# Graph attention on one core: query rows ordered by their number of edges

## The chip, the core and the metric

The kernel runs on one core of a Trainium2 chip. The core has a matrix engine (TensorE, in the profile PE, with its weight loads as PEld), a vector engine (VectorE, DVE), a scalar engine (ScalarE, ACT), a general engine (GpSimd, POOL), an engine that only issues transfers here (SyncE, SP) and 16 DMA engines. Each engine works through its own queue of instructions in order; semaphores tie the queues together. The metric is the device time of one execution in microseconds (us), taken as the median of several runs. Less is better.

## The reference

One layer of graph attention with a residual and a layer norm, all in float32. x is 16 x 1024 x 512: 16 batches of 1024 nodes. adj is one 1024 x 1024 matrix of zeros and ones that all batches share. With 8 heads of 64 columns:

```python
q, k, v = (x @ Wq + bq), (x @ Wk + bk), (x @ Wv + bv)      # each split into 8 heads of 64
scores = einsum('bqhd,bkhd->bhqk', q, k) / 8
scores = scores + (1.0 - adj) * -1e9                       # only edges count
out = einsum('bhqk,bkhd->bqhd', softmax(scores), v)
y = x + out @ Wo + bo
y = (y - mean(y)) / sqrt(var(y) + 1e-5)                    # over the 512 columns
```

adj is sparse and uneven: 4043 edges in all, up to 66 in one row, and 60 rows with none (such a row attends to all nodes alike).

## The kernel before

**Edges instead of a dense matrix.** The kernel doesn't compute all scores. It puts 128 query rows on the 128 partitions (a tile; 8 tiles, t = 0 to 7, in a batch) and works in blocks of one edge per partition. A block gathers, for each partition, the key and value row of that edge (`kvg`, 4 KB a row, an indirect DMA from POOL out of `kv_rows` in device memory), multiplies query and key (`products`, DVE), reduces each head's 64 products (`scores`, DVE), takes the exponential (`exponentials`, ACT) and multiplies the value row by it (`weigh`, on ACT as eight instructions or on DVE as one, as `by_act` says).

**Two kinds of block.** A tile's *own* blocks (OWN[t] of them) hold one edge of each of its own 128 queries, so the query tile `qt` serves them all, and the weighted rows are added in place on DVE (`add_own`). Rows with more edges leave a remainder. These are packed, 128 to a *shared* block (BLOCKS[t] of them); there each partition's query row has to be gathered as well (`qg`, a second indirect DMA), and a 0/1 matrix (`sums`) adds the rows to their queries by two matmuls (`add_up`, TensorE). A batch has 21 own and 15 shared blocks, 36 in all, 576 in the run. `normalise` adds the two sums, divides by the sum of exponentials, and the result is transposed.

**Everything else.** For each batch `pair` computes q, k and v for two tiles at a time on TensorE (k and v by seven products in place of eight, with weights prepared in T1 to T4) and stores them as rows (`q_rows`, `kv_rows`, three batches deep). `norm` squares q and k per head on ACT and keeps the sums: at the end `guard` checks with them that the exponentials, which are taken without subtracting a maximum, stayed within LIMIT, and otherwise a plain program recomputes all. `finish` takes a tile through the output product, adds x (`load_y`) and bo (on POOL), takes mean and variance (the power on POOL) and stores the rows.

**Order.** The order of each engine's instructions is written out by a loop over steps, one block a step (n). At step n it gathers block n + 8, multiplies block n + 4 and reduces it, takes the exponential of block n + 3, weighs block n + 2 (ACT) or n + 1 (DVE) and adds block n. TensorE's other work, and the work that follows from it, is handed out by a credit (`share`) worked out from the costs PRODUCT, SUM and TRANSPOSE, so that every step gets an equal part of it. 34 steps (LEAD_IN) run before block 0; in them the weights are prepared and the edge lists made (`edges`, one list per tile, started at the steps EDGES_FROM). After the last q, k and v, ten tiles' attention results that were put aside (SPILL) are brought back and finished.

**Queues.** SP issues the plain transfers: x, the stores of q and kv rows, `qt` (128 contiguous rows of `q_rows`), `y` (128 rows of x again) and the output rows. POOL issues the indirect ones: `kvg` and `qg`. In its queue also stand the bias addition on `y` and the power of the variance.

The functions that the change touches, with their callers:

Of the kernel before, what the change touches and what calls it, by code (L numbers as in the profile page):

```python
# [16 lines left out]
HEADS = 8  # L17
EPS = 1e-5
NEG = 1e9
LIMIT = 28.0  # L20
# [3 lines left out]
OWN = (7, 3, 3, 1, 1, 2, 2, 2)  # L24
BLOCKS = (5, 2, 1, 2, 2, 1, 1, 1)
DEGREE = (80, 16, 16, 16, 16, 16, 16, 16)

AHEAD = 8
KG_BUFS, QG_BUFS, QT_BUFS, PV_BUFS = 8, 4, 3, 5
# [10 lines left out]
EDGES_FROM = (-33, -30, -18, -14, -10, -5, 0, 5)  # L40
# [111 lines left out]
def kernel(  # L152
# [33 lines left out]

    nc = tc.nc
# [30 lines left out]
    with ExitStack() as main:  # L218
# [6 lines left out]
        def fill_psum(name):  # L225
# [21 lines left out]
            one.tile([P, 2, D], F32, name=name) for name in ("b11", "b21", "b22", "t1", "t2", "t3", "t4")  # L247
# [8 lines left out]
        check = one.tile([P, 2 * NT], F32, name="check")  # L256
        gmax = one.tile([P, 2 * B], F32, name="gmax")

        kv_rows = [dram.tile([N + 1, 2 * D], F32, name=f"kv_rows_{i}") for i in range(ROWS)]
        q_rows = [dram.tile([N, D], F32, name=f"q_rows_{i}") for i in range(ROWS)]  # L260
        spill = [dram.tile([P, D], F32, name=f"spill_{i}") for i in range(len(SPILL))]
# [36 lines left out]
        def bias_setup():  # L298
            bk_bc = work.tile([P, D], F32, tag="y", name="bk_bc", bufs=4)
            broadcast(bk_bc, bk)  # L300
            yield
            n8 = small.tile([P, HEADS], F32, name="bk_norms")
            nc.vector.tensor_tensor(bk_bc, bk_bc, bk_bc, op=OP.mult)
            nc.vector.tensor_reduce(n8, bk_bc.rearrange("p (h d) -> p h d", d=HD), axis=AX.X, op=OP.add)
            nc.vector.tensor_reduce(bk_norm, n8, axis=AX.X, op=OP.max)
# [8 lines left out]
            bvb = work.tile([P, NPAIR, P], F32, tag="y", name="bvb", bufs=4)  # L314
# [19 lines left out]

        def edges(t):
            nb, J, K = BLOCKS[t], DEGREE[t], OWN[t]
            a = work.tile([P, N], F32, tag="kv", name=f"a_{t}", bufs=5)
            nc.sync.dma_start(a, adj[ds(t * P, P), :])
            for _ in range(3):
                yield  # L340
            v = work.tile([P, N], F32, tag="kv", name=f"codes_{t}", bufs=5)
            nc.gpsimd.tensor_tensor(v, a, place[:, 0:N], op=OP.mult)
            st = small.tile([P, 4], F32, name="est")
            deg, end, lim, off = (st[:, i:i + 1] for i in range(4))
            kl = small.tile([P, J + 2], F32, tag=f"kl{J}", name=f"kl_{t}", bufs=2)
            kr = small.tile([P, max(OWN)], F32, tag="kr", name=f"kr_{t}", bufs=2)
            yield

            nc.scalar.activation(a, a, AF.Copy, accum_out=deg)
            nc.scalar.activation(a, a, AF.Square, bias=neg_one, scale=2.0)  # L350
            nc.scalar.activation(a, a, AF.Square, bias=neg_one, accum_out=check[:, t:t + 1])
# [21 lines left out]
            nc.vector.tensor_scalar(deg, deg, -float(K), 0.0, op0=OP.add, op1=OP.max)  # L373
# [6 lines left out]
            nc.vector.tensor_copy(kl[:, J + 1:J + 2], query[:, t:t + 1])  # L380
# [5 lines left out]
            of = work.tile([P, max(BLOCKS) * P], F32, tag="of", name=f"of_{t}", bufs=1)  # L386

            o, span = of[:, 0:nb * P], place[:, 0:nb * P]
# [27 lines left out]
            for i0 in range(0, nb, 4):  # L416
# [7 lines left out]
                )  # L424

# [51 lines left out]
        def norm(b, t, i, s):  # L477
            if t == 0 and i == 0:
                NRM[b] = work.tile([P, 2, NT, HEADS], F32, tag="nrm", name=f"nrm_{b}", bufs=2)
            for h in range(HEADS):  # L480
                sq = work.tile([P, HD], F32, tag="sq", name=f"sq_{b}_{t}_{i}_{h}", bufs=2)
                nc.scalar.activation(sq, s[:, ts(h, HD)], AF.Square, accum_out=NRM[b][:, i, t, h:h + 1])  # L482
# [156 lines left out]
        def load_y(b, t, tag="y", bufs=4):  # L639
            Y[b, t] = work.tile([P, D], F32, tag=tag, name=f"y_{b}_{t}", bufs=bufs)  # L640
            loaded[b, t] = now[0]
            nc.sync.dma_start(Y[b, t], x[b, ds(t * P, P), :])

            if fronts or t % 2:
                later(2 if fronts else 3, lambda: nc.gpsimd.tensor_tensor(Y[b, t], Y[b, t], bo_bc, op=OP.add))  # L645
                biased[b, t] = True

        def reload(b, t, k):
            OT[b, t] = work.tile([P, D], F32, tag="ewg"[k % 3], name=f"oTs_{b}_{t}", bufs=1)
            nc.sync.dma_start(OT[b, t], spill[b * NT + t - SPILL[0]])  # L650
            load_y(b, t, "q", 2)
# [343 lines left out]
```

## Time and profile before

| | us |
|---|---|
| median of three runs (lowest to highest) | 2121.68 (2117.72 to 2123.0) |
| the profiled execution | 2120.32 |
| its span, first to last instruction | 2118.5 |

| engine | busy us | share of the span |
|---|---|---|
| TensorE (PE) | 2034.2 | 96% |
| VectorE (DVE) | 1930.0 | 91% |
| ScalarE (ACT) | 1642.2 | 78% |
| GpSimd (POOL) | 1196.2 | 56% |

The DMA engines moved 583.25 MB. The software queue q0, fed by POOL, took 47.0% of their time, and the hardware queue q1, fed by SP, 31.9%. The mean granted clock of TensorE was 0.987.

How to read it: a busy share is an average over the span; a matmul's end is modelled, so neighbours overlap; a float32 matmul is recorded as two. An indirect DMA on POOL shows the time in which POOL makes it, not the transfer. In a group's row the idle time in front names what ended it. Issues on SP don't count as busy time.

### The profile page before, as it was taken

To read this page: it belongs to the slowest core of one execution; us is meant where nothing else is said; L and a number is where in the kernel's file an instruction comes from. 1 tells how busy PE (TensorE), PEld (TensorE's weight loads), DVE (VectorE), ACT (ScalarE), POOL (GpSimd) and SP (SyncE) were. 2 spreads that over 40 slices of the span, in tenths; PEclk is the share of its full clock that TensorE was granted. 3 is DMA by queue.
4 is the path that set the end of the run, shared out by engine and by line. 5 is a ranking of instruction groups with operands and counts; after the bars stand their busy time and mean duration, and the time that the engine had idled before them with its cause. 6 is when DMAs were issued, how large, how long until landed. Compare 5 with 4: busy or idle time off the path is not lost. (4 is left out here: it accounts for less than half of the span.)

```text
span 2118.5 us, 29525 instructions
## 1 busy us (share of the span) xinstructions
PE 2034.2 (96%) x5933; PEld 1031.0 (49%) x5933; DVE 1930.0 (91%) x3860; ACT 1642.2 (78%) x8132; POOL 1196.2 (56%) x1098
## 2 busy tenths in 40 slices
PE   8897999999999999999999999999999999999677
PEld 3444555454554545545554555555455554554343
DVE  6789999999989899998999999999989989999876
ACT  5477888777878788787877878787887869897665
POOL 2044566655656565565655656465555656566872
PEclk9998999999999999999999999999999999999889
DMA  5367788787978878797887879878787988989883
GB/s 194 110 232 237 266 285 318 265 323 250 337 248 294 286 258 325 241 314 260 279 314 243 324 243 320 281 270 317 243 327 238 329 274 300 325 309 328 284 310 112
DMA packets 219596, 583.25 MB, mean 275 GB/s; under 512 B 34047, under 2 KB 34059, under 8 KB 219406
## 3 DMA queue, kind: packets, MB, share of 16 engines
q0 software_dynamic: 102144, 331.89, 47.0%
q1 hardware_dynamic: 114656, 244.40, 31.9%
q10 hardware_dynamic: 2606, 4.99, 0.7%
q14 instruction: 141, 1.16, 0.2%
q8 instruction: 49, 0.80, 0.1%
HBM read 477.37 MB, written 136.88 MB: 290 GB/s over the span
## 5 line engine op out<-in xcount | busy, mean ns | idle before, releaser
L722 POOL DMA_INDIRECT kvg<-kv_rows,key_row x576 | 641.0, 1113 | 413.0 <-DVE pv L767 132.3
L763 ACT ACTIVATE pv<-kvg,pv 128x64 f32<-128x64 f32 x2624 | 660.7, 338 | 0.2 <-ACT pv L753 0.2
L470 PE MATMUL pq<-wq,xT 128*128 128x512 f32 x1024 | 481.7, 596 | 3.8 <-DVE y L663 3.7
L470 PE MATMUL po<-wo,oT 128*128 128x512 f32 x944 | 431.5, 596 | 0.7 <-ACT oT L811 0.7
L743 DVE TENSOR_REDUCE s<-qk 128x8 f32<-128x512 f32 x576 | 390.8, 678 | 6.4
L716 POOL DMA_INDIRECT qg<-q_rows,query_row x240 | 273.2, 1138 | 76.7 <-issue 62.7
L470 PEld LDWEIGHTS pq<-wq,xT 128*128 128x128 f32 x1024 | 189.3, 191 | 199.3 <-issue 176.8
L470 PEld LDWEIGHTS po<-wo,oT 128*128 128x128 f32 x944 | 179.7, 192 | 201.6 <-issue 189.8
L482 ACT ACTIVATE sq<-q 128x64 f32<-128x64 f32 x1024 | 245.5, 244 | 37.8 <-DVE q L497 37.8
L739 DVE TENSOR_TENSOR qk<-qt,kvg 128x512 f32<-128x512 f32 x336 | 261.0, 777 | 0.0
L676 POOL TENSOR_TENSOR stats<-stats,neg_half 128x1 f32<-128x1 f32 x128 | 88.2, 689 | 288.1 <-DVE stats L675 283.4
L482 ACT ACTIVATE sq<-kv 128x64 f32<-128x64 f32 x1024 | 245.3, 244 | 3.8 <-ACT sq L482 3.1
L586 PE MATMUL x<-b,xT 128*128 128x512 f32 x504 | 238.4, 595 | 0.1
L586 PE MATMUL pp<-t,s 128*128 128x512 f32 x504 | 237.1, 593 | 0.7 <-DVE w L602 0.7
L482 ACT ACTIVATION_READ_ACCUMULATOR sq<-kv 128x1 f32 x1024 | 195.2, 191 | 0.0
L482 ACT ACTIVATION_READ_ACCUMULATOR sq<-q 128x1 f32 x1024 | 194.6, 190 | 0.0
L645 POOL TENSOR_TENSOR y<-y,bo_bc 128x512 f32<-128x512 f32 x116 | 161.5, 1393 | 41.4 <-DMA y<-in_x_dram 40.2
L779 DVE TENSOR_TENSOR pv<-pv,pv 128x520 f32<-128x520 f32 x208 | 179.0, 860 | 0.5 <-ACT pv L763 0.5
L739 DVE TENSOR_TENSOR qk<-qg,kvg 128x512 f32<-128x512 f32 x240 | 174.1, 725 | 5.2 <-issue 4.2
L753 ACT ACTIVATE pv<-s,absent 128x8 f32<-128x8 f32 x336 | 95.8, 293 | 102.3 <-DVE o L796 70.0
L767 DVE TENSOR_TENSOR pv<-kvg,pv 128x512 f32<-128x512 f32 x248 | 174.5, 703 | 0.0
L788 PE MATMUL sum<-pv,sums 128*128 128x256 f32 x480 | 146.7, 388 | 19.0 <-DVE pv L767 14.5
(149 smaller groups left out, 2972.9 us busy)
## 6 DMA issues: line engine op xcount, KB each, us to landing
kv_rows<-kv SPq DMA_DIRECT2D x128, 512.0 KB
x<-in_x_dram SPq DMA_DIRECT2D x128, 256.0 KB
q_rows<-q SPq DMA_DIRECT2D x128, 256.0 KB
qt<-q_rows SPq DMA_DIRECT2D x128, 256.0 KB
y<-in_x_dram SPq DMA_DIRECT2D x128, 256.0 KB
out_dram<-y SPq DMA_DIRECT2D x128, 256.0 KB
kvg<-kv_rows,key_row POOLq DMA_INDIRECT x576
a<-in_adj_dram SPq DMA_DIRECT2D x8, 512.0 KB
```

The costliest lines, as they stand in the source:

```text
L470: nc.tensor.matmul(p, lhs()[:, ts(c, P)], w[:, c, :], start=(c == 0), stop=(c == NPAIR - 1))
L482: nc.scalar.activation(sq, s[:, ts(h, HD)], AF.Square, accum_out=NRM[b][:, i, t, h:h + 1])
L586: nc.tensor.matmul(R[bank], l[:, ts(c, P)], right[:, c, :], start=(first and c == 0), stop=(c == 1), skip_group_check=True,)
L645: later(2 if fronts else 3, lambda: nc.gpsimd.tensor_tensor(Y[b, t], Y[b, t], bo_bc, op=OP.add))
L716: nc.gpsimd.indirect_dma_start(out=QG[n], out_offset=None, in_=q_rows[b % ROWS], in_offset=bass.IndirectOffsetOnAxis(ap=query_row[:, g:g + ...
L722: nc.gpsimd.indirect_dma_start(out=KG[n], out_offset=None, in_=kv_rows[b % ROWS], in_offset=bass.IndirectOffsetOnAxis(ap=key_row[:, g:g + ...
L739: nc.vector.tensor_tensor(QK[n], q, KG[n][:, 0:D], op=OP.mult)
L743: nc.vector.tensor_reduce(S[n], QK.pop(n).rearrange("p (h d) -> p h d", d=HD), axis=AX.X, op=OP.add)
L763: nc.scalar.activation(pv[:, ts(h, HD)], v[:, ds(D + h * HD, HD)], AF.Copy, scale=pv[:, D + h:D + h + 1])
L767: nc.vector.tensor_tensor(pv[:, 0:D].rearrange("p (h d) -> p h d", d=HD), v[:, D:].rearrange("p (h d) -> p h d", d=HD), pv[:, D:, None].to ...
L779: nc.vector.tensor_tensor(PV[b, t], PV[b, t], pv, op=OP.add)
L788: nc.tensor.matmul(PSUM[b, t][:, 0, 0:HD2], m, pv[:, 0:HD2], **kw)
```

## The change

**Order by degree.** A new preparation, `ranks`, loads all eight tiles of adj, sums each row on ACT, ranks the 1024 rows by degree (a row-wide comparison per tile on DVE, with the row number breaking ties), and scatters (row, degree) to its rank in device memory by eight indirect DMAs. Read back, `asked_row[:, t]` names the 128 rows of tile t. From then on a tile is 128 rows of like degree. `edges` gathers its rows of adj by that list, and `qt`, `y` and the output rows, which are no longer contiguous, become indirect DMAs on POOL.

**Other blocks.** OWN becomes (1, 2, 2, 3, 4, 5, 5, 7) and BLOCKS (0, 0, 0, 0, 0, 0, 1, 5): 29 own and 6 shared blocks a batch, 35 in all, 560 in the run. Tiles 0 to 5 have no sum on TensorE, and `normalise` takes their sums as they are. The matrices and offsets are made for two tiles only.

**Norms of pairs.** `norm` takes one sum for two heads, 128 columns, so four ACT instructions with an accumulator in place of eight; the sum of a pair bounds each head's, and LIMIT goes from 28 to 31.

**Smaller edits.** `by_act` gives every second block with i = 0 to ACT in all batches, where before it did so in the first and last only. `qt` and `pv0` get one buffer more, `y` five in place of four; reloaded tiles use the storage of T1 to T4 for y, and up to three of them may be open. The store of the output comes two steps after the last ACT instruction, before it one. The check that adj holds only zeros and ones moves into `checks`, and the value buffers are cleared there.

```diff
-OWN = (7, 3, 3, 1, 1, 2, 2, 2)
-BLOCKS = (5, 2, 1, 2, 2, 1, 1, 1)
-DEGREE = (80, 16, 16, 16, 16, 16, 16, 16)
+OWN = (1, 2, 2, 3, 4, 5, 5, 7)
+BLOCKS = (0, 0, 0, 0, 0, 0, 1, 5)
+DEGREE = (8, 8, 8, 8, 8, 8, 16, 80)
-KG_BUFS, QG_BUFS, QT_BUFS, PV_BUFS = 8, 4, 3, 5
+KG_BUFS, QG_BUFS, QT_BUFS, PV_BUFS, Y_BUFS = 8, 4, 4, 5, 5
-EDGES_FROM = (-33, -30, -18, -14, -10, -5, 0, 5)
+EDGES_FROM = (-14, -13, -12, -10, -8, -4, -6, -15)
...
+        def ranks():
+            for _ in range(2):
+                yield
+            for t in range(NT):
+                ADJ.append(work.tile([P, N], F32, tag="kvg", name=f"adj_{t}", bufs=KG_BUFS))
+                nc.gpsimd.dma_start(ADJ[t], adj[ds(t * P, P), :])
...
+            for t in range(NT):
+                nc.scalar.activation(ADJ[t], ADJ[t], AF.Copy, accum_out=asked[:, t, 1:2])
...
+            for t in range(NT):
+                nc.vector.scalar_tensor_tensor(
+                    keys, row, key[:, t:t + 1], place, op0=OP.is_lt, op1=OP.min, accum_out=rank[:, t:t + 1]
+                )
...
+            for t in range(NT):
+                nc.gpsimd.indirect_dma_start(
+                    out=order_views[t], out_offset=bass.IndirectOffsetOnAxis(ap=rank_row[:, t:t + 1], axis=0),
+                    in_=asked[:, t, :], in_offset=None,
+                )
+            for _ in range(2):
+                yield
+            nc.sync.dma_start(ranked, order.rearrange("(t p) c -> p t c", p=P))
+            yield
+            nc.vector.tensor_copy(asked_row, ranked[:, :, 0])
...
         def norm(b, t, i, s):
...
-            for h in range(HEADS):
-                sq = work.tile([P, HD], F32, tag="sq", name=f"sq_{b}_{t}_{i}_{h}", bufs=2)
-                nc.scalar.activation(sq, s[:, ts(h, HD)], AF.Square, accum_out=NRM[b][:, i, t, h:h + 1])
+            for h in range(NPAIR):
+                sq = work.tile([P, P], F32, tag="sq", name=f"sq_{b}_{t}_{i}_{h}", bufs=2)
+                nc.scalar.activation(sq, s[:, ts(h, P)], AF.Square, accum_out=NRM[b][:, i, t, h:h + 1])
...
         def load_y(b, t, k=None):
...
-            nc.sync.dma_start(Y[b, t], x[b, ds(t * P, P), :])
+            nc.gpsimd.indirect_dma_start(
+                out=Y[b, t], out_offset=None, in_=x_rows,
+                in_offset=bass.IndirectOffsetOnAxis(ap=asked_row[:, t:t + 1], axis=0), element_offset=b * N * D,
+            )
...
                 def norm_out():
                     nc.scalar.activation(y, y, AF.Identity, bias=st[:, 4:5], scale=st[:, 3:4])
-                    later(1, store)
+                    later(2, store)

                 def store():
-                    nc.sync.dma_start(out_ap[b, ds(t * P, P), :], y)
+                    nc.gpsimd.indirect_dma_start(
+                        out=out_rows[b, t], out_offset=bass.IndirectOffsetOnAxis(ap=asked_row[:, t:t + 1], axis=0),
+                        in_=y, in_offset=None, element_offset=b * N * D,
+                    )
...
         def gather(n):
...
-                nc.sync.dma_start(QT[b, t], q_rows[b % ROWS][ds(t * P, P), :])
+                nc.gpsimd.indirect_dma_start(
+                    out=QT[b, t], out_offset=None, in_=q_rows[b % ROWS],
+                    in_offset=bass.IndirectOffsetOnAxis(ap=asked_row[:, t:t + 1], axis=0),
+                )
...
         def by_act(n):
             b, t, i = blocks[n]
-            return 0 < i < OWN[t] or ((b in (0, B - 1) or i >= OWN[t]) and n % 2 == 0)
+            return 0 < i < OWN[t] or n % 2 == 0
...
         def normalise(b, t):
...
+            if BLOCKS[t]:
+                s = PSUM.pop((b, t))
+                nc.vector.tensor_tensor(r, s[:, 1, HD2:HD2 + HEADS], pv[:, D:], op=OP.add)
...
+            else:
+                nc.vector.reciprocal(r, pv[:, D:])
```

## The prediction

> **What bounds the kernel now.** I read the page first: the shares by engine and the forty slices.
>
> ```profile
> PE 2034.2 (96%) x5933; PEld 1031.0 (49%) x5933; DVE 1930.0 (91%) x3860; ACT 1642.2 (78%) x8132; POOL 1196.2 (56%) x1098
> ...
> PE   8897999999999999999999999999999999999677
> ```
>
> TensorE is busy from the third slice to the last three. The busy time of a stretch that leaves out the start and the end, and of the last stretch, came next (columns: stretch, length, busy us and instructions of PE, PEld, DVE, ACT, POOL, then clock, DMA share, GB/s).
>
> ```profile
> 383.00:1757.00 1374.00, 1367.70 (x4020) 695.72 (x4019) 1273.57 (x2488) 1090.59 (x5495) 803.12 (x737) 1.00 0.83 284
> ...
> 1966.00:2079.00 113.00, 80.27 (x215) 40.97 (x214) 95.82 (x230) 79.23 (x279) 79.81 (x81) 0.88 0.83 280
> ```
>
> From 383 to 1757 us eleven batches (2 to 12) take 1374 us, 124.9 each, and TensorE is busy 99.5% of that at full clock: the bound. DVE follows at 93%. In the last batch no engine is full: chains decide. The batch limits are the starts of every 36th reduction of line 743; they give 138 us for batch 0, 115 for batch 1, 109 and 111 for batches 13 and 14, and 142 us from the first reduction of batch 15 to the end.
>
> Third, the groups by form (mean ns of one, then idle before it).
>
> ```profile
> L763 ACT ACTIVATE pv<-kvg,pv 128x64 f32<-128x64 f32 x2624 | 660.7, 338 | 0.2 <-ACT pv L753 0.2
> L722 POOL DMA_INDIRECT kvg<-kv_rows,key_row x576 | 641.0, 1113 | 413.0 <-DVE pv L767 132.3 <-ACT pv L753 97.4 <-issue 82.6
> ...
> L716 POOL DMA_INDIRECT qg<-q_rows,query_row x240 | 273.2, 1138 | 76.7 <-issue 62.7 <-DVE qk L739 11.9 <-DVE s L743 0.9
> ...
> L482 ACT ACTIVATE sq<-q 128x64 f32<-128x64 f32 x1024 | 245.5, 244 | 37.8 <-DVE q L497 37.8
> ...
> L779 DVE TENSOR_TENSOR pv<-pv,pv 128x520 f32<-128x520 f32 x208 | 179.0, 860 | 0.5 <-ACT pv L763 0.5
> ...
> L645 POOL TENSOR_TENSOR y<-y,bo_bc 128x512 f32<-128x512 f32 x116 | 161.5, 1393 | 41.4 <-DMA y<-in_x_dram 40.2
> L789 PE MATMUL sum<-pv,sums 128*128 128x264 f32 x480 | 148.8, 392 | 0.5 <-ACT pv L763 0.5
> L788 PE MATMUL sum<-pv,sums 128*128 128x256 f32 x480 | 146.7, 388 | 19.0 <-DVE pv L767 14.5 <-DVE rden L800 4.5
> ```
>
> Then the waits, and POOL in order of time (start, us, what).
>
> ```profile
> POOL stats L676 <- DVE stats L675: 283.4, 87, 5.2
> ```
>
> ```profile
> 902.84 0.97 POOL L716 DMA_INDIRECT qg<-q_rows,query_row  x1 [0.30 <-issue]
> 904.11 1.48 POOL L722 DMA_INDIRECT kvg<-kv_rows,key_row  x1 [0.30 <-issue]
> 905.90 0.96 POOL L716 DMA_INDIRECT qg<-q_rows,query_row  x1 [0.30 <-DVE pv L779]
> ```
>
> POOL's idle time is mostly waiting because it is early. Back to back, an indirect DMA costs its own 1.12 us plus 0.30 us of gap: 1.42 us. That number decides this case.
>
> **What the Trainium skill says.** Perfetto Trace Analysis, "DMA Instruction — SWDGE (GPSIMD)": such an interval is the generation of descriptors, not the transfer, so the 1.12 us is POOL's own work; the trace agrees, since its packet records, matched in order to the 816 issues, put the last packet at a median 5.0 us (2 KB rows) and 5.5 us (4 KB rows) after the issue. DMA: Bandwidth & Descriptors, "SWDGE vs HWDGE vs iDMA": all these DMAs go through one software queue; here it is q0, 47.0% of the DMA engines. SBUF — State Buffer, "Who interferes with whom": a DVE instruction with two SBUF inputs contends with a GpSimd instruction that reads SBUF. The trace agrees for line 645, which reaches 911.67:
>
> ```profile
> 910.47 1.76 DVE L779 TENSOR_TENSOR pv<-pv,pv 128x520 f32<-128x520 f32 x1
> ...
> 913.42 0.69 DVE L779 TENSOR_TENSOR pv<-pv,pv 128x520 f32<-128x520 f32 x1
> ```
>
> Such stretching adds 113 us to DVE in all, while of 1,937 DVE instructions beside an indirect DMA alone two were stretched. So more indirect DMAs should not slow DVE, and the bias additions stay (118 for 116).
>
> **The change, part by part.**
>
> *TensorE.* Sums go from 15 to 6 blocks a batch. The busy rows give 295.5/240 = 1.23 us a block, but ends are modelled; from the first matmul of a block to the next instruction is 0.88 us (median). I take 0.88, low end of the two: 9 x 0.88 = 7.9 us a batch, 127 us in all. The other end is 11.1. A TensorE-bound batch becomes 124.9 - 7.9 = 117.0.
>
> *DVE.* Products +128 x 0.777 - 144 x 0.725 = -5; weighing -136 x 0.703 = -96; additions +128 x 0.860 = +110; reductions -16 x 0.678 = -11; normalising without a sum in 96 tiles -96 x (0.680 + 0.156) = -80; shorter edge lists and the new ranks about -17. Sum -99: 1831 us, 107 us a batch. Not shown before: the 1024-wide comparison of the ranks; nearest row 1.46 us (L356), 8 of them, in the sum.
>
> *ACT.* 120 more blocks weighed: 960 x 0.252 (660.7/2624, they overlap) = +242. Norms now take 881 us for 2048 squares with their accumulator reads. A 128-wide square isn't in the trace; VectorE: DVE Perf Modes, "The TRN2 errata", prices ACT at 224 cycles plus the width at 1.2 GHz, 0.240 us for 64 (row: 0.244), so 0.29 estimated for 128; by the slope to line 672 (0.717 for 512), 0.31. With the 0.19 read, 1024 x 0.50 = 512: -369. Sum with exponentials -119: 1523 us.
>
> *POOL, where it is paid.* The queries are no longer contiguous rows, so loads of qt and y and stores of out, 128 each, move from SP's hardware queue to indirect DMAs; 144 qg and 16 kvg gathers go. Net +224 x 1.42 = +318 us. A steady batch has 65 such DMAs for 51: 65 x 1.42 + 8 x 1.39 + 8 x 0.69 = 109 us, against 89 of 124.9 before. Still under 117, at 93%. But it is uneven. In the changed order of POOL, steps 0 to 13 hold 21 DMAs, 30 us of work in 47; steps 14 to 34 hold 44 DMAs, 8 biases and 8 powers: 62.5 + 11.1 + 5.5 = 79 us in 21 x 3.34 = 70. POOL ends some 9 us late. It can be 7.7 late: a gather now precedes its reduction by 15.2 us (median), at the least 7.5. Queued behind are the gathers, and DVE's products wait for those. Line 645 also waits for a y now landing 5 us after issue from a late POOL. I take 2.5 us a batch lost: 119.5.
> The scatter of out has no row. Low end 0.97 like the shortest gather; high end 2.16, the longest in the trace, 8 us a batch more, which alone lifts POOL to 117. I take 1.12.
> SP loses 392 issues and keeps x, q_rows and kv_rows, which nothing then delays.
>
> *Costed at nothing.* The fifth y buffer, fourth qt, third pv0 and the store one step later only loosen waits; the columns named "idle before" show none on these tiles. If they are still too few, POOL stands at a y load until the store five tiles back has landed, with the gathers behind it.
>
> *Transfers.* -37.7 MB of qg; kvg rows unchanged, as each edge and each isolated node is one row (4103 a batch). 100 MB move from q1 to q0. Hidden; uncovered, a late gather is the case above.
>
> *Start.* All 4 MB of adj are asked for at once beside 3 MB of wq and wk, wv. The first 17 us now move about 5 MB, near 310 GB/s, so I add 6 us (between 0 and 12: 3.5 MB at that rate is 11). The chain of ranks (eight scatters of 1.4 us, two landings) fits about four lead-in steps; if not, DVE and SP stand a few us at it.
>
> *End.* Batches 13 and 14 run at DVE 95-97%: -6.5 each, -13. Last batch: POOL's order from its first gather to the end holds 34 kvg, 6 qg, 7 qt, 19 y, 31 out, 12 biases, 28 powers. Here I use 1.3 us back to back (the undisturbed 1.0 + 0.3), 0.65 for a power: 126 + 16 + 18 = 160 us, as long as POOL takes now from there (1956.9 to 2118.5), waits not counted. I add 12 (between -7, were POOL hidden, and +30).
>
> Sum on the span of 2118.5: 6 - 13 x 5.4 - 13 + 12 = -65, so 2053; the execution's own time was 2120.3, 1.8 above its span, so **2055 us**. The median of the runs, 2121.7, is 0.06% above that execution.
>
> **Rivals.**
> - *TensorE alone.* POOL's lateness stays within the slack: 117.0 a batch, 4 - 13 x 7.9 - 14 - 7 = -120, 2000 us. For it: 93% is under 100%, and DVE and ACT get lighter in every batch. Against: POOL's heavy 21 steps.
> - *POOL sets the batch (slower).* One cost, the indirect DMA on POOL with what it waits for. 65p + 16.6 = 124.9 at p = 1.67 us, 0.25 above the measured start to start. At 1.85 a batch is 137: +156, and with start and end about 2290. For it: 1.48 and 2.16 us intervals exist, and every y and out adds a wait for a buffer or for ACT. Against: mean 1.12.
> - *Little gained.* POOL at 1.55 to 1.65, or the start and end eat it: 2095 to 2130.
>
> **How the numbers follow.** Forecast (own range 2020 to 2090) 0.45; TensorE alone 0.20; little gained 0.15; POOL sets the batch 0.20. A change of 0.3% (6 us) is about what a measurement can tell. Faster: 0.45 + 0.20 + 0.09 = 0.74; same 0.05; slower 0.21. The range 1990 to 2145 takes in the first three and the nearer part of the POOL case.
>
> **What the profile after would show.** Right: reductions of line 743's kind 117 to 121 us apart every 35; POOL near 70% busy with its waits for the power (283 us now) mostly gone; ACT near 1520, DVE near 1830; idle time of DVE and TensorE behind gathers near each batch's end. Wrong: indirect DMAs longer than 1.25 us in the mean, POOL without idle time, a tail over 160 us, or a first gather much later than 122 us.

## The result: the changed kernel, and its profile

The changed kernel takes 2144.0 us, the median of four runs (2132.54 to 2148.86), against 2119.7 for the kernel before (2117.72 to 2123.0): a ratio of 1.0105, interval 1.0061 to 1.0149. It is 1% slower, and its fastest run is slower than the slowest of the kernel before. The profiled execution took 2142.24 us with a span of 2140.5, 22 us more than the 2118.5 before.

The page of the changed kernel, shares by engine and one of the slice rows:

```profile
PE 1946.7 (91%) x5334; PEld 930.5 (43%) x5334; DVE 1810.1 (85%) x3545; ACT 1686.2 (79%) x7024; POOL 1474.0 (69%) x1350
...
PE   8968999999999999999999999999999999998664
```

TensorE lost 88 us of work and DVE 120, and yet the span grew. The share that rose is POOL's, from 56% to 69%; ACT's rose by one point. The last four slices of the PE row fell from "9677" to "8664".

Windows of the changed kernel: batches 2 to 11, and most of the last stage (columns as before: length, PE, PEld, DVE, ACT, POOL, clock, DMA share, GB/s):

```profile
392.00:1637.00 1245.00, 1189.98 (x3295) 571.73 (x3296) 1083.16 (x2111) 1032.87 (x4359) 900.49 (x811) 0.98 0.79 266
...
1986.00:2110.00 124.00, 76.49 (x174) 34.83 (x173) 91.97 (x212) 88.15 (x314) 99.31 (x104) 0.83 0.68 215
```

TensorE is busy 95.6% of the steady batches, where it was 99.5%, and its clock is 0.98, where it was 1.00: it is still the fullest engine, but now it waits. In the last stage POOL, busy 99 of 124 us with a gap before each of its DMAs, is the fullest engine.

The groups of the changed kernel that answer to the rows shown before:

```profile
L850 ACT ACTIVATE pv<-kvg,pv 128x64 f32<-128x64 f32 x3584 | 902.7, 339 | 1.6 <-remote 1.6
L809 POOL DMA_INDIRECT kvg<-kv_rows,key_row x560 | 638.0, 1139 | 306.5 <-issue 107.4
L793 POOL DMA_INDIRECT qt<-q_rows,asked_row x128 | 144.7, 1130 | 35.9 <-issue 35.0
L767 POOL DMA_INDIRECT out_dram<-y,asked_row x128 | 144.8, 1132 | 34.7 <-issue 22.1
L720 POOL DMA_INDIRECT y<-in_x_dram,asked_row x128 | 143.2, 1118 | 32.0 <-issue 31.7
L557 ACT ACTIVATE sq<-q 128x128 f32<-128x128 f32 x512 | 150.7, 299 | 13.7 <-DVE q L572 13.4
```

The durations are those of the prediction: 1.12 to 1.14 us for every kind of indirect DMA, the scatter of `out` included. No kind of instruction on POOL became clearly dearer (`kvg` rose most, from 1.113 to 1.139 us).

The waits of the changed kernel (who waited, for whom; us in all, times, longest):

```profile
POOL stats L757 <- DVE stats L756: 78.4, 38, 5.0
DVE y L744 <- POOL y L726: 62.8, 27, 6.2
DVE qk L826 <- DMA kvg<-kv_rows,key_row: 46.3, 12, 7.3
DVE stats L760 <- POOL stats L757: 46.1, 33, 6.3
```

The direction has turned. Before, POOL stood 283 us at the power, waiting for DVE; now 78. And DVE, which stood 10.5 us at a power and 9.9 at a bias addition in the kernel before,

```profile
DVE stats L679 <- POOL stats L676: 10.5, 8, 3.9
DVE y L663 <- POOL y L645: 9.9, 4, 5.4
```

stands 46 and 63, and 46 more at gathered rows.

Where the 22 us lie, by stages. The limits are the starts of every 36th reduction of scores (every 35th in the changed kernel), "start" is the time of the first and "last" is from the first reduction of batch 15 to the end of the span.

| us | start | batch 0 | batch 1 | batches 2 to 12, each | batch 13 | batch 14 | last |
|---|---|---|---|---|---|---|---|
| before | 130.2 | 138.0 | 115.3 | 124.9 | 108.5 | 110.9 | 141.8 |
| changed | 141.7 | 137.6 | 113.5 | 124.0 | 103.6 | 125.8 | 153.9 |
| difference | +11 | 0 | -2 | -0.9 | -5 | +15 | +12 |

The forecast had +6, -5.4 in each of batches 0 to 12, -6.5 in each of 13 and 14, and +12. Two terms are far off: the steady batch (-12 in all instead of -70) and batch 14.

### The profile page after: what moved, and what is told of

It is laid out like the page before. It is cut to its first block, busy times and chain, and to the rows that moved or that the text cites. A ratio compares the mean times of both kernels' runs of the same rounds, so it can differ in the third digit from the quotient of the medians.

```text
span 2140.5 us, 26366 instructions
## 1 busy us (share of the span) xinstructions
PE 1946.7 (91%) x5334; PEld 930.5 (43%) x5334; DVE 1810.1 (85%) x3545; ACT 1686.2 (79%) x7024; POOL 1474.0 (69%) x1350
## 5 line engine op out<-in xcount | busy, mean ns | idle before, releaser
L850 ACT ACTIVATE pv<-kvg,pv 128x64 f32<-128x64 f32 x3584 | 902.7, 339 | 1.6 <-remote 1.6
L826 DVE TENSOR_TENSOR qk<-qt,kvg 128x512 f32<-128x512 f32 x464 | 355.6, 766 | 52.4 <-DMA kvg<-kv_rows,key_row 43.7
L753 ACT ACTIVATE ysq<-y,stats 128x512 f32<-128x512 f32 x128 | 91.9, 718 | 113.9 <-DVE stats L749 107.9
L793 POOL DMA_INDIRECT qt<-q_rows,asked_row x128 | 144.7, 1130 | 35.9 <-issue 35.0
L767 POOL DMA_INDIRECT out_dram<-y,asked_row x128 | 144.8, 1132 | 34.7 <-issue 22.1
L720 POOL DMA_INDIRECT y<-in_x_dram,asked_row x128 | 143.2, 1118 | 32.0 <-issue 31.7
L557 ACT ACTIVATE sq<-q 128x128 f32<-128x128 f32 x512 | 150.7, 299 | 13.7 <-DVE q L572 13.4
L557 ACT ACTIVATE sq<-kv 128x128 f32<-128x128 f32 x512 | 150.6, 299 | 0.0
L661 PEld LDWEIGHTS x<-b,xT 128*128 128x128 f32 x504 | 96.0, 193 | 118.7 <-issue 109.1
L661 PEld LDWEIGHTS pp<-t,s 128*128 128x128 f32 x504 | 95.0, 192 | 110.3 <-issue 101.9
```

Source lines behind the costliest of these rows:

```text
L557: nc.scalar.activation(sq, s[:, ts(h, P)], AF.Square, accum_out=NRM[b][:, i, t, h:h + 1])
L661: nc.tensor.matmul(R[bank], l[:, ts(c, P)], right[:, c, :], start=(first and c == 0), stop=(c == 1), skip_group_check=True,)
L720: nc.gpsimd.indirect_dma_start(out=Y[b, t], out_offset=None, in_=x_rows, in_offset=bass.IndirectOffsetOnAxis(ap=asked_row[:, t:t + 1], axi ...
L767: nc.gpsimd.indirect_dma_start(out=out_rows[b, t], out_offset=bass.IndirectOffsetOnAxis(ap=asked_row[:, t:t + 1], axis=0), in_=y, in_offse ...
L793: nc.gpsimd.indirect_dma_start(out=QT[b, t], out_offset=None, in_=q_rows[b % ROWS], in_offset=bass.IndirectOffsetOnAxis(ap=asked_row[:, t: ...
L826: nc.vector.tensor_tensor(QK[n], q, KG[n][:, 0:D], op=OP.mult)
```

## The steady batch: what eats 7 us

TensorE's work allows 117.0 us a batch and the batch takes 124.0. The trace offers two suspects. They meet at the border between two batches, where DVE stands longest. The steps (one reduction to the next, means over batches 2 to 12) show it: they are 1.9 to 5.1 us long, but the one into a new batch takes 7.9 us, with DVE busy for 2.9 of them. POOL in order of time at such a border of the changed kernel, with the DVE instruction it ends at:

```profile
1386.75 1.02 POOL L809 DMA_INDIRECT kvg<-kv_rows,key_row  x1 [1.28 <-DMA kv_rows<-mean]
1388.07 1.24 POOL L793 DMA_INDIRECT qt<-q_rows,asked_row  x1 [0.31 <-issue]
1389.62 1.00 POOL L809 DMA_INDIRECT kvg<-kv_rows,key_row  x1 [0.30 <-ACT pv L850]
1390.93 1.00 POOL L809 DMA_INDIRECT kvg<-kv_rows,key_row  x1 [0.30 <-ACT sq L557]
1391.96 0.58 POOL L757 TENSOR_TENSOR stats<-stats,neg_half 128x1 f32<-128x1 f32 x1
1392.51 1.26 POOL L726 TENSOR_TENSOR y<-y,bo_bc 128x512 f32<-128x512 f32 x1
1392.57 1.23 DVE L760 TENSOR_TENSOR stats<-stats 128x1 f32<-128x1 f32 x1 [3.36 <-POOL stats L757]
```

The first gather of the new batch waits for that batch's last row (`kv_rows<-mean`); three DMAs follow with only the usual 0.30 us between them, and the power and the bias addition stand behind them. DVE waits 3.36 us for the power, and what stands behind it in DVE's queue waits with it.

- **Late rows.** A gather is asked for eight steps before its block. In the kernel before, the new batch's rows are complete nine steps ahead; in the changed one six to seven. The constant `EARLY` (11 steps), from which `share` sets how far TensorE's q, k and v work runs ahead, is the same in both, but the work between is not. So the first gathers of a batch leave late and in a bunch. They precede their reductions by 7.5, 8.2, 9.4 and 8.7 us in the mean (before: 14.0, 14.3, 20.6 and 16.1).
- **A full POOL.** 90 us busy a batch, and 65 gaps of 0.30 us before a DMA, make 109 of 124. A bunch that has formed has little room in which to dissolve.

**A second place.** DVE's longest stand isn't yet TensorE's loss. TensorE itself stands 5.2 us of each steady batch, and 2.1 of them lie at the border, in its step and the eight after it. Another 2.5 lie in the middle of the batch, between the 18th and the 20th reduction, and there it is one wait, the largest in total that TensorE has in this run:

```profile
PE pxT L516 <- DVE y L744: 27.5, 10, 4.7
```

One of the ten, with the DVE instruction that ends it and the POOL instruction before that:

```profile
824.96 1.27 POOL L726 TENSOR_TENSOR y<-y,bo_bc 128x512 f32<-128x512 f32 x1
...
826.26 0.69 DVE L744 SCALAR_TENSOR_TENSOR y<-po,y 128x512 f32<-128x512 f32 x1 [2.38 <-POOL y L726]
...
827.02 1.12 PE L516 MATMUL pxT<-ident,x 128*128 128x128 f32 x4 [4.69 <-DVE y L744]
```

In all ten the `y` of DVE begins 0.03 to 0.04 us after POOL's bias addition has ended, and POOL had made that addition straight after an indirect DMA or a power, without idle time. So the full queue shows here too, but what comes late is a bias, not a gather.

The experiments take away late rows, POOL's work, both, or neither but something that only looks like them.

### Rows earlier: EARLY 14, then EARLY 13

```diff
-EARLY = 11
+EARLY = 14
```

> The changed kernel with EARLY 14 in place of 11: TensorE's q, k and v of the next batch are planned three steps earlier, so that their rows are complete 9 steps before the batch's first block and not 6, and its first gathers go out 8 steps ahead and not 5 or 6. POOL has the same instructions. Theory 1 (POOL's queue is too full whatever the order): within 10 us of the changed kernel's 2144. Theory 2 (the rows of the next batch come too late, so that its first gathers are bunched and DVE stands some 5 us in the last step of each batch): about 5 us in each of 12 batches comes back, 2080 to 2095.

2108.14 us, ratio 0.9955 (0.9938 to 0.9972). This kernel leaves out the end of the last tile (one output store of 128), so only its steady batches are used: 121.1 us each, against 124.0. That is less than the second theory asked for (2080 to 2095), but part of the 7 us is the late rows. With 13 steps nothing is left out:

```diff
-EARLY = 11
+EARLY = 13
```

> The changed kernel with EARLY 13 alone, the bias still on POOL; rows of the next batch complete 8 steps ahead. If the late rows and POOL's work are separate costs that add up: 1.2 us a batch back, as between the two kernels with the bias on DVE (117.9 and 116.7): about 2128. If the late rows only hurt because POOL is full: more, 121 to 122 us a batch, 2105 to 2120.

2086.97 us, ratio 0.9854 (0.9836 to 0.9872), more than expected: one constant turns 1% slower into 1.5% faster. A steady batch takes 118.4 us. DVE's waits in this kernel:

```profile
DVE stats L760 <- POOL stats L757: 66.0, 46, 4.8
DVE y L744 <- POOL y L726: 64.7, 24, 4.2
DVE qk L826 <- DMA kvg<-kv_rows,key_row: 10.5, 14, 2.2
```

The wait for gathered rows fell from 46.3 to 10.5 us, and the two waits for POOL's own work did not fall. So the 5.6 us a batch did not come from a quicker power or bias. TensorE's idle time falls from 5.2 to 1.9 us a batch: at the border from 2.1 to 0.1, and at the wait for DVE's `y` from 2.5 to 0.4, although DVE stands at the bias almost as long as before (46 us in batches 2 to 12, in the changed kernel 53). Why TensorE is then so seldom behind it isn't shown. Why 14 does worse than 13 in the steady batches stays open too; with 14, TensorE idles 3.1 us a batch, 0.2 of them at the border.

### POOL relieved: bias additions on DVE

```diff
-            if fronts or t % 2:
+            if False:
                 later(2 if fronts else 3, lambda: nc.gpsimd.tensor_tensor(Y[b, t], Y[b, t], bo_bc, op=OP.add))
```

DVE then adds bo itself, with an instruction more for each of those tiles.

> The changed kernel with the addition of bo to y done by DVE (a second instruction in the output step, 0.6 us) and not by POOL. POOL loses 118 instructions of 1.35 us, DVE its 45 us of waits for them in batches 2 to 11 and the stretching beside them, and gains about 80 us of work. Theory 1: POOL has 10 us a batch less, 2090 to 2115. Theory 2: the late rows stay, 2135 to 2150.

2055.17 us, ratio 0.9691 (0.9672 to 0.971), far better than either theory had it. A steady batch takes 117.9 us. The rows are as late as in the changed kernel: DVE still waits 42.9 us for gathered rows and still stands at the border. TensorE's wait in the middle of the batch is gone, and its idle time is 1.2 us a batch, 1.1 of them at the border. So taking 10.8 us (8 x 1.35) from POOL does as much as bringing the rows earlier, although it puts 0.7 us an instruction on DVE.

### POOL relieved further: plain transfers

```diff
-                nc.gpsimd.indirect_dma_start(
-                    out=QT[b, t], out_offset=None, in_=q_rows[b % ROWS],
-                    in_offset=bass.IndirectOffsetOnAxis(ap=asked_row[:, t:t + 1], axis=0),
-                )
+                nc.sync.dma_start(QT[b, t], q_rows[b % ROWS][ds(t * P, P), :])
```

and likewise for `y` and `out`: the three streams go back to SP's queue. That leaves out the order of the query rows in these three, while blocks and edge lists stay as they are, so the work on every other engine is that of the changed kernel.

> The changed kernel with qt, y and the output rows as plain transfers on SP again, as in the kernel before: 24 indirect DMAs a batch leave POOL. Left out: the order of the query rows (a tile's qt, x and output rows are those of the plain order, beside edge lists of the new order), the bytes are the same. Theory 1: POOL falls from 109 to 75 us a batch, TensorE's 117 us a batch become the bound, and what is left of the loss is the start (11 us): 2000 to 2025. Theory 2: with 5 or 6 steps of lead, 16 us or more, the gathers are late only because they are bunched; without POOL's other DMAs at most half of the 5 us a batch comes back and nothing else: 2100 to 2120. If neither POOL nor the order of gathers is the cause (TensorE's clock, or the dependence of DVE and ACT on each other with more own blocks): 2130 to 2145.

2031.05 us, ratio 0.9579 (0.9563 to 0.9595), 6 us above the range of the first theory. A steady batch takes 118.4 us, no less than with the bias alone, and not the 117 of that theory. The last stage takes 127.6 us instead of 153.9: here is where the additional DMAs on POOL do cost time of their own.

### Both: bias on DVE and EARLY 13

```diff
-EARLY = 11
+EARLY = 13
...
-            if fronts or t % 2:
+            if False:
```

> The changed kernel with the bias addition on DVE and EARLY 13 (the rows of the next batch complete 8 steps ahead, first gathers 7). With the bias on DVE alone batches 2 to 11 took 117.9 us each, and DVE still stood 35 us at gathered rows in eleven batches. If the late rows are what remains: 117.0 a batch, TensorE's own time, and 2040 to 2050. If the two causes are one (once POOL has room, 5 steps of lead do): 2050 to 2060, no difference.

2048.8 us, ratio 0.9674 (0.9656 to 0.9692), the fastest of the kernels that compute all: 3.3% below the kernel before and 4.4% below the changed one (2048.8/2144.0). A steady batch takes 116.7 us. Window of its steady batches:

```profile
392.00:1600.00 1208.00, 1207.16 (x3426) 587.64 (x3425) 1118.00 (x2267) 1063.16 (x4505) 818.86 (x755) 1.00 0.84 285
```

TensorE is busy 1207 of 1208 us at full clock: the bound of 117.0 that the prediction worked out is reached and holds. Nothing lies below it: all of it together, plain transfers, bias on DVE and EARLY 13, gives the same.

> The changed kernel with the bias on DVE, EARLY 13, and qt, y and the output rows as plain transfers on SP. Left out: the order of the query rows (plain rows beside edge lists of the new order; the bytes are the same). POOL has 41 indirect DMAs a batch, 61 us of work. If TensorE is the only bound of the steady batches that is left: 116.5 to 117 a batch, no better than with POOL's 98 us, and all the gain over 2049 is in the last two batches, 25 to 40 us: 2005 to 2025. If POOL still costs something in the steady batches: below 116 a batch.

2007.63 us, ratio 0.9481 (0.9464 to 0.9499), 116.5 us a steady batch with POOL at 541 of 1208 us. POOL is early again: it stands 273 us at the power, waiting for DVE.

Against the kernel with both and indirect DMAs, the remaining time (44 us of span) lies mostly at the end: 231.9 us for batch 14 and the last stage, against 267.8.

| steady batch, us | step into a new batch | DVE idle in it | TensorE idle in the batch | batch |
|---|---|---|---|---|
| changed | 7.9 | 5.0 | 5.2 | 124.0 |
| EARLY 14 | 4.3 | 0.3 | 3.1 | 121.1 |
| EARLY 13 | 5.7 | 1.5 | 1.9 | 118.4 |
| plain transfers | 6.7 | 4.0 | 1.5 | 118.4 |
| bias on DVE | 6.6 | 4.2 | 1.2 | 117.9 |
| bias on DVE, EARLY 13 | 4.3 | 1.1 | 0.3 | 116.7 |
| the same, plain transfers | 3.3 | 0.2 | 0.2 | 116.5 |

(The steps are those that end batches 2 to 12.) The batch follows TensorE's idle time and not DVE's stand at the border: with the bias on DVE, or with plain transfers, that stand stays nearly whole, and the batch is short all the same; with EARLY 14 it is almost gone, and the batch is longer than with 13.

Undoing one cause gains 5.6 or 6.1 us, undoing both 7.4. They do not add, and could not, since about 116.5 us is TensorE's own time; either one alone takes away three quarters of the loss. That fits a loss which needs both, late rows and a queue too full to work the bunch off. The last of the controls below says the same from another side.

### Is it POOL's time, or that DVE depends on the bias?

The bias on DVE takes away two things: POOL's time, and DVE's wait for POOL's addition (62.8 us). This kernel gives the time back without the dependence: POOL fills a spare tile that nobody reads.

```diff
-            if fronts or t % 2:
-                later(2 if fronts else 3, lambda: nc.gpsimd.tensor_tensor(Y[b, t], Y[b, t], bo_bc, op=OP.add))
-                biased[b, t] = True
+            if (fronts or t % 2) and now[0] > 20:
+                later(2 if fronts else 3, lambda: [nc.gpsimd.memset(before, 0.0) for _ in range(SPARE)])
```

> The changed kernel with the bias addition on DVE, and nine memsets of a spare 128 x 128 tile at the place on POOL where it stood, for which nothing waits (1.0 to 1.5 us in all, to be read from the trace). If it is POOL's time that the bias takes from the gathers: back to 122 to 126 us a batch, 2110 to 2150. If it is DVE waiting for the bias and being held up beside it: it stays at 118 a batch, 2050 to 2070.

2205.31 us, ratio 1.0412 (1.0391 to 1.0433), and 128.0 us a steady batch. One such filling, in the order of time:

```profile
945.73 2.31 POOL L727 MEMSET before<- 128x128 f32 x9
```

It came out longer than the addition it stands for, 2.3 us in the mean against 1.35, so it puts some 18 us a batch on POOL where the bias put 10.8. So time on POOL costs by itself, with nothing waiting for the filling. How much of the 6.1 us it explains isn't settled: a straight line from 117.9 (none) to 128.0 (18) passes 10.8 at 123.9, and the changed kernel has 124.0, but no run with 10.8 shows that the line is straight, and in the changed kernel's trace TensorE's largest wait hangs on the bias. DVE now waits at the power instead:

```profile
DVE stats L760 <- POOL stats L757: 180.7, 73, 12.9
```

### More time for the power

```diff
-                later(3, shift)
-                later_last(4, norm_out)
+                later(5, shift)
+                later_last(6, norm_out)
```

> The changed kernel with DVE's use of the power two steps later (the shift at step 5 and ACT's last instruction at step 6 after the output product, not 3 and 4). POOL's work is the same, only DVE no longer waits for a power that stands behind gathers. Theory 1, if the waits for small POOL results are the larger part of it: 2115 to 2130; if the late gathers are: 2135 to 2150, as theory 2 has it.

2147.94 us, ratio 1.0132 (1.0115 to 1.0149): no gain. A steady batch takes 123.7 us, and the end grows. Giving DVE's read of the power two steps more does not help while POOL's queue itself is late. DVE's waits only move: in batches 2 to 12 it stands 71.6 us at the bias, where it stood 53 in the changed kernel. The first gathers of a batch lead their reductions by 7.0 to 9.1 us, as in the changed kernel.

### Controls: one part at a time on the kernel before

The bias additions on DVE, in the kernel before:

```diff
-            if fronts or t % 2:
+            if False:
```

> The kernel before with the bias addition on DVE, a control: there TensorE is busy 99.5% of batches 2 to 12 and POOL has 35 us a batch to spare. All theories of POOL: within 0.3% of 2119, since only DVE's work grows, from 113 by about 5 less the stretching of up to 6 us a batch. If the bias on POOL hurt in itself, whatever POOL's load: faster, 2070 to 2100.

2108.64 us, ratio 0.9946 (0.9929 to 0.9964). I expected no difference, and there is a small gain of 11 us, told of at the end. It lies between the two ranges, and is an eighth of what the same edit gains in the changed kernel (89 us), so the large gain belongs to the change.

The three streams as indirect DMAs in the kernel before, with its own blocks and row order:

```diff
-                nc.sync.dma_start(QT[b, t], q_rows[b % ROWS][ds(t * P, P), :])
+                nc.gpsimd.indirect_dma_start(
+                    out=QT[b, t], out_offset=None, in_=q_rows[b % ROWS],
+                    in_offset=bass.IndirectOffsetOnAxis(ap=asked_row[:, t:t + 1], axis=0),
+                )
```

and likewise for `y` and `out`, with the store one step later.

> The kernel before with qt, y and the output rows as indirect DMAs on POOL (rows in plain order, the result is the same) and the store two steps later, as in the change: that part of the change alone, with the old blocks. POOL then has 75 x 1.42 + 16.6 = 123 us of work in a batch of 124.9. If POOL's work is the cause: 130 to 140 us a batch with its waits, 2190 to 2330. If it was the late rows (which this kernel doesn't have: 9 steps ahead): below 2150.

2228.49 us, ratio 1.0515 (1.0497 to 1.0532). The steady batch takes 127.2 us, less than expected: it holds 75 indirect DMAs (51 + 24), and 75 x 1.42 + 16.6 = 123 us of POOL in 127. POOL is fuller here than in the changed kernel, whose share is 109 of 124, and yet the batch is only 2.3 us over TensorE's 124.9: with rows nine steps ahead, and the blocks of the kernel before, a full queue costs little in the steady batches. Of the 109 us that the whole run loses, 26 are in batches 2 to 12 and 65 in the last stage, 206.5 us instead of 141.8. So the order by degree, which drops nine `qg` gathers and one `kvg` from each batch, pays for part of the DMAs that it requires.

## The ends

Batch 14 was costed by DVE and forecast at -6.5; it came at +15. A window of about that batch, changed kernel:

```profile
1860.20:1986.00 125.80, 110.77 (x295) 51.74 (x294) 105.89 (x208) 95.87 (x400) 92.43 (x89) 0.96 0.82 277
```

72 indirect DMAs start in it, where the kernel before starts 54: 39 `kvg`, 10 `qt`, 6 `qg`, 11 `y`, 6 `out`. With their gaps, 92.4 + 72 x 0.30 = 114 of 126 us of POOL. With bias on DVE and EARLY 13 the same stage takes 120.6 us, and with plain transfers besides 109.3, with POOL at 53.8: 11 us go with those DMAs. It is the computation of the last stage, which the prediction had made, that was missing one stage earlier: there too the finishing of tiles catches up.

The last stage was forecast at +12, by 160 us of POOL, and came at +12 and 153.9. To move its work forward I let only six tiles be put aside in place of ten:

```diff
-SPILL = range(102, 112)
+SPILL = range(106, 112)
...
-            while n < total or plan or rest or urgent or done or finishing or spilled:
+            while n <= total or plan or rest or urgent or done or finishing or spilled:
```

on top of bias on DVE and EARLY 13.

> The changed kernel with the bias on DVE, EARLY 13, and six finished tiles put aside for the end, not ten (and the loop over steps kept running for its last block). Four tiles' loads, stores and finishing move from the last batch and a half, where POOL is full, to batch 13, where it has 58 us of work in 104. If POOL's queue sets the end: 10 to 20 us less at the end for about 5 more in batch 13, 2030 to 2045. If not, TensorE's 14 us more in batch 13 is a loss: 2050 to 2065.

2051.66 us, ratio 0.9689 (0.9668 to 0.9711): nothing gained. The last stage is 6.8 us shorter and batch 14 1.7, and batch 13 is 12.9 longer: TensorE is busy for all of its 114.3 us and has no room for those tiles.

The start came at +11 and was forecast at +6, between 0 and 12. No experiment took it apart. In the trace of the changed kernel DVE is busy 19.3 of the last 20 us ahead of the first reduction (141.7), above all with the edge lists of tiles that have two and three own blocks, and earlier the first weight matmuls and the list of ranks wait for transfers; which of these sets the +11 stays open.

## The norms of pairs

This kernel undoes them, on top of bias on DVE and EARLY 13:

```diff
-            for h in range(NPAIR):
-                sq = work.tile([P, P], F32, tag="sq", name=f"sq_{b}_{t}_{i}_{h}", bufs=2)
-                nc.scalar.activation(sq, s[:, ts(h, P)], AF.Square, accum_out=NRM[b][:, i, t, h:h + 1])
+            for h in range(HEADS):
+                sq = work.tile([P, HD], F32, tag="sq", name=f"sq_{b}_{t}_{i}_{h}", bufs=2)
+                nc.scalar.activation(sq, s[:, ts(h, HD)], AF.Square, accum_out=NRM[b][:, i, t, h:h + 1])
```

> The changed kernel with the bias on DVE, EARLY 13, and the norms of single heads again, 16 ACT instructions a tile and not 8. ACT gains about 370 us of work, 23 a batch, on 102 to 105 busy of 117. If ACT has room only because of the norms of pairs: ACT becomes the bound at 124 to 128 us a batch, 2140 to 2220. If its busy time overstates it: 2049 to 2070.

2094.62 us, ratio 0.9892 (0.987 to 0.9913), between the two ranges; a steady batch takes 119.4 us, less than the 124 to 128 of ACT as the bound. ACT, first in the kernel with pairs (bias on DVE, EARLY 13):

```profile
PE 1918.5 (94%) x5334; PEld 925.2 (45%) x5334; DVE 1806.0 (88%) x3663; ACT 1681.3 (82%) x7024; POOL 1313.6 (64%) x1232
```

and with single heads:

```profile
PE 1936.1 (92%) x5334; PEld 926.4 (44%) x5334; DVE 1805.8 (86%) x3663; ACT 1858.5 (89%) x9072; POOL 1325.0 (63%) x1232
```

The pairs take 177 us from ACT, not the 369 of the prediction, and are worth 46 us of time here (2094.62 - 2048.8). The reason for the wrong size is in the trace of the kernel before, on ACT:

```profile
900.58 0.24 ACT L482 ACTIVATE sq<-q 128x64 f32<-128x64 f32 x1
900.72 0.19 ACT L482 ACTIVATION_READ_ACCUMULATOR sq<-q 128x1 f32 x1
900.81 0.24 ACT L482 ACTIVATE sq<-q 128x64 f32<-128x64 f32 x1
```

The read of the accumulator begins 0.14 us after its square and ends with the next square under way: from square to square it is 0.24 us, not 0.24 + 0.19. Pairs stand 0.29 to 0.30 apart. So 2048 x 0.24 - 1024 x 0.295 = 189 us, close to the 177 measured.

## Why the prediction was wrong, step by step

- **The bound of TensorE** (117.0 a batch, 0.88 us a block of sums): right. 116.7 and 116.5 in the two kernels in which nothing else is in the way.
- **Prices on POOL** (1.42 us start to start; 109 us a batch; the scatter at 1.12): right. Steady POOL is 90 + 65 x 0.30 = 109 us. The rival in which POOL sets the batch, at 1.67 us and over, did not occur: the batch is nearly as long as that rival's threshold, 124.9, for another reason.
- **Late by 9 us with 7.7 to spare, so 2.5 us lost**: this is the step that failed. The term is 7.0 us a batch, not 2.5: the 124.0 measured, less the 117.0 of TensorE's own work. The place was named in part, the end of each batch, where gathers queue behind POOL's other work. Two things in the step were wrong.
  - *The 7.7 us to spare.* They were read from the kernel before, as the lead of a gather over its reduction (15.2 us in the median, at least 7.5). But that lead is itself set by when the new batch's rows are complete, and the change moved that, too, from nine to six or seven steps ahead, while `EARLY` stayed. At the first step of a batch the lead was 14.0 us in the mean before; in the changed kernel it is 7.5, and 6.1 at the least. A gather of 4 KB rows lands 5.5 us after its issue by the prediction's own figure, so there was hardly anything to spare. Rows two steps earlier give 5.6 of the 7.0 us back. (The 2.5 doesn't follow from 9 and 7.7 either, which leave 1.3; it was taken with something added for the waits.)
  - *What waits.* The sum lets DVE's products wait for gathers. In the changed kernel TensorE's largest wait is for a DVE that has stood at a bias addition in the middle of the batch.
- **What a wait costs.** Of TensorE's 124.0 us a batch, 118.9 are busy (2.5 more than the 116.4 of the kernel that runs without waits) and 5.2 idle. The larger busy time goes with the clock of 0.98. The Trainium skill, TensorE: Matmul & The Clock Gate, "What's actually happening", says that the clock falls to half after an idle window and takes about 3.4 us of work to return. The trace agrees: batches 2 to 12 have nine stretches at half clock, six of 3.4 us and three of 6.8, and each begins no more than 1.4 us from the end of a wait of TensorE of 1.9 to 4.7 us, seven of them at the wait for DVE's `y`. (Not every such wait is followed by one: 2.5 us before 891.91 were not.) The four transposes after the wait shown above take 1.12 us; the four just before it, at 821.73, took 0.60. The nine stretches are 3.7 us a batch, and half of that, by estimate 1.9 us, is most of the 2.5. So a wait can be paid for twice.
- **"Line 645 also waits for a y ... from a late POOL"**: right as a wait (DVE stands 62.8 us at the bias), and given no number of its own. How much of the 7.0 it makes isn't settled: moving the addition gives 6.1 us back, but takes POOL's time away together with the wait, and the spare filling shows that POOL's time costs by itself.
- **DVE's sum** (-99; 1831 us): came at 1810. Additions were priced at 0.860 us and took 0.722 in the mean. The 107 us a batch doesn't follow from the sum, which gives about 110 (115.8 before, less 6); the trace has 108.2.
- **ACT's sum** (-119; 1523 us): wrong, it came at +44 and 1686 us. The price of one square was good (0.29 estimated, 0.299 measured) and that of weighing too (0.252), but the reads of the accumulator were counted although they overlap. With 189 us saved on norms, 242 added for weighing and 11 for exponentials it would have been +64. ACT stayed under TensorE, so this didn't decide.
- **Transfers hidden**: right. The two queues took 75% of the DMA engines, and with plain transfers the steady batch is no shorter than with the bias moved.
- **Start** +6: came at +11, inside the range given. **Batches 13 and 14**, -6.5 each: -5 and +15. The second was costed by DVE alone; POOL's 72 DMAs were not counted. **Last stage**, +12: right, +12.

With 7.0 for 2.5, +15 for -6.5 and +11 for +6, the prediction's own sum gives 11 - 13 x 0.9 - 6.5 + 15 + 12 = +20; the span grew by 22. The rival "little gained" ended at 2130; the result lies beyond it, at the very end of the range (2145), by a cost that the forecast had named and taken too small.

## What to carry to other kernels

A lead or a slack that is read from a profile belongs to the order of work in that profile: before spending it, ask what sets it, and whether the change moves that as well. When a queue becomes nearly full, look at its worst few steps in a row and at what must happen before them, not at its mean, and at which instruction the bounding engine stands, not only the engine that feeds it; here one constant that starts the producers two steps earlier was worth 57 us. And when work moves to another engine's queue, count that queue in every stage, the last but one included.

## What the runs showed of the hardware that was not expected

**A small gain from moving POOL's additions to DVE, in the kernel before.** DVE does 116 instructions more, and yet its busy time in the steady batches falls from 1273.57 to 1260.79 us. TensorE, the bound there, idles 0.6 us a batch in the kernel before and less than 0.1 in this one: 6 of the 11 us; 5 more are in the last stage. Two groups of this kernel (bias on DVE):

```profile
L739 DVE TENSOR_TENSOR qk<-qt,kvg 128x512 f32<-128x512 f32 x336 | 229.6, 683 | 0.0
...
L779 DVE TENSOR_TENSOR pv<-pv,pv 128x520 f32<-128x520 f32 x208 | 144.0, 692 | 2.1 <-ACT pv L763 2.1
```

With the additions on POOL the same two groups took 261.0 and 179.0 us (the second row is among the prediction's):

```profile
L739 DVE TENSOR_TENSOR qk<-qt,kvg 128x512 f32<-128x512 f32 x336 | 261.0, 777 | 0.0
```

So 66 us of stretching went with the additions in these two groups alone, not far from the 80 us that 116 additions on DVE cost at 0.69 us. The Trainium skill, SBUF — State Buffer, "Who interferes with whom", has the contention of DVE's instructions with two SBUF inputs with GpSimd's reads; the prediction took the stretching as unchanged, since the additions stay. That they cost DVE at least as much from POOL as they would on DVE itself is what it didn't see: over the whole run DVE's busy time falls by 21 us, although 116 additions came to it.

**A scatter by index costs POOL what a gather costs:** 1.13 us for `out`, 1.12 for `y`, 1.13 for `qt`, 1.14 for `kvg` with rows twice as long. After the last one, though, 11 us pass to the end of the span (it starts at 2129.47 of 2140.5), against 6 after the last plain store of the kernel before (2112.1 of 2118.5).
